# Moving the bfloat16 conversion of quantised x, with its row sums, from ScalarE to one accumulating VectorE instruction per token tile

## Chip, cores and metric

The kernel runs on one core of one Trainium2 chip. The metric is the device time in microseconds from launch to end, as the median of several runs of the same program. One more execution is recorded by the hardware profiler; the views quoted below come from it.

The engines are called PE (TensorE matmuls; PEld is its weight load), DVE (VectorE), ACT (ScalarE), POOL (GpSimd) and SP (SyncE, which only issues transfers here).

## The reference

Input x is 2 x 1024 x 2048 in float32, ctx is 2 x 2048 x 2048. There are two layers with residuals:

```
q(t, s, z) = (clip(round(t / s + z), 0, 255) - z) * s
x = x + q(layernorm(x), s1, z1) @ q(ctx, s2, z2)
z = layernorm(x)
x = x + z @ W + bias + per-group LoRA(z) + shared LoRA(z)
```

The second layer has a 2048 x 2048 weight W, and eight groups of 256 tokens whose LoRA matrices are mixed by a gate.

The kernel forms the first product on centred integers. With c1 = q-integer of x minus 128 and c2 = q-integer of ctx minus 128, it computes c1 @ c2 in bfloat16 (both fit exactly) and corrects for zero points other than 128: a column term from the sums of c2, and a row term from the sums of c1 over a token's 2048 features. The row sums are what accompanies the changed conversion.

## The kernel before, in words

The two batches are done one after the other. Tokens of a batch are eight tiles of 128 rows (`MT = 8`); two tiles make a group of 256 tokens (`MG = 2`, four groups), whose x stays in SBUF as `y[g]` throughout.

**Preparing a tile of x**, `prep_x(b, m, ...)`: DVE takes statistics in four pieces (`st1`, L279), a chain of 128x1 operations makes mean and reciprocal deviation (L253 to L265, with a square root on ACT, L257), then a scale `k` and an offset `o` (L283 to L286). ACT quantises the whole 128 x 2048 tile to uint8, `q8` (L291). ACT then converts `q8` to centred bfloat16, `qh`, in two halves of 1024 columns, each writing its row sums into a column of `rsum` (L294). PE transposes each half in eight 128 x 128 blocks into a PSUM tile (`pt`, L299), and DVE copies that into the operand `c1T` (L300). DVE adds the two row sums (L303) and multiplies by a constant into `r_s` (L304). `q8` alternates between two places in the working buffer `wk`, by parity of m; `qh` has only one place there. `pt`, the column term's `pc` and other small PSUM tiles share a pool of two buffers (`ps_m`).

**Preparing ctx**, `quantise`: ACT scales and rounds a 128 x 2 x 512 piece to int16 (L310), DVE clips and centres it to bfloat16 (L313). Eight pieces make one block of 512 columns. `column_term` sums them on PE (L327) and DVE scales the sums (`bp`, L329).

**The product**, `xattn_pair(b, n, g)`: for each of the two tiles of a group ACT preloads a PSUM accumulator with column term plus row term (L340, needs `r_s`), PE runs 16 matmuls on it (L342), and then DVE scales and adds the accumulator to `y` (L351) and takes statistics for the second layer norm (L353). Three accumulators rotate. Sixteen pairs make a batch's first layer.

**The second layer** (`ffn`) is computed in float32 with two nested seven-product schemes (L580), with operands combined on DVE and POOL and the results added to `y` (L598). While batch 0's last stage of it runs, `meanwhile` already loads and prepares tiles 0 to 3 of batch 1 and the first two column blocks of ctx. Tiles 4 to 7 of batch 1 are prepared after it, between the first pairs of batch 1.

**Order of the work.** Each engine executes its instructions in the order in which it got them. The order is settled ahead of the run by the framework's planner, which takes the order of the program text as priority and works with estimated durations; the preload L340 is marked as of high priority. Loads of x and ctx are issued from SP, in a list (`todo`) that moves on as buffers are given back after L310. Semaphores between engines are made by the framework from the tiles that instructions read and write.

Of the kernel before, what the change touches and what calls it, by code (L numbers as in the profile page):

```python
# [10 lines left out]
F32 = mybir.dt.float32  # L11
# [3 lines left out]
AF = mybir.ActivationFunctionType  # L15
ALU = mybir.AluOpType
# [4 lines left out]
P = 128  # L21
# [5 lines left out]
CENTRE = 128.0  # L27
# [39 lines left out]
def tile_quant_xattn_then_lora_ffn(  # L67
# [17 lines left out]
    nc = tc.nc  # L85
    B, S, D = x.shape
    KT = D // P
    MT = S // P
# [9 lines left out]
    H = D // 2  # L98
# [5 lines left out]
    small = ctx.enter_context(tc.tile_pool(name="small", bufs=4))  # L104
# [21 lines left out]
    r_s = const.tile([P, MT], F32, tag="r_s", name="r_s")  # L126
# [13 lines left out]
    def flat(t):  # L140
        return t.rearrange("p k n -> p (k n)")
# [67 lines left out]
    s12, d1, d2, kdd = (k_s[:, i : i + 1] for i in range(4))  # L209
    n_centre = const.tile([P, 1], F32, tag="n_centre", name="n_centre")  # L210
# [39 lines left out]
    def norm_stats(stats, name):  # L250

        mv = small.tile([P, 2], F32, tag="mv", name=f"mv_{name}")
        nc.vector.bn_aggr(mv, stats.rearrange("p n s -> p (n s)"))  # L253
        ve = small.tile([P, 1], F32, tag="ve", name=f"ve_{name}")
        nc.vector.tensor_scalar_add(ve, mv[:, 1:2], EPS)
        sd = small.tile([P, 1], F32, tag="sd", name=f"sd_{name}")
        nc.scalar.activation(sd, ve, AF.Sqrt)  # L257
        r0 = small.tile([P, 1], F32, tag="r0", name=f"r0_{name}")
        nc.vector.reciprocal(r0, sd)

        t = small.tile([P, 1], F32, tag="nt", name=f"nt_{name}")
        nc.vector.scalar_tensor_tensor(t, ve, r0, r0, ALU.mult, ALU.mult)
        nc.vector.tensor_scalar(t, t, -0.5, 1.5, ALU.mult, ALU.add)
        rstd = small.tile([P, 1], F32, tag="rstd", name=f"rstd_{name}")
        nc.vector.tensor_mul(rstd, r0, t)  # L265
        return mv[:, 0:1], rstd
# [6 lines left out]
    def prep_x(b, m, c1T, wk):  # L273

        nm = f"{b}_{m}"
        g, tok = m // MG, ds((m % MG) * P, P)
        ym = y[g][:, m % MG, :]
        for n in range(NN):
            nc.vector.bn_stats(st1[:, m, n, :], ym[:, ds(n * NB, NB)])  # L279
        mean, rstd = norm_stats(st1[:, m], f"a{nm}")  # L280

        k = small.tile([P, 1], F32, tag="kx", name=f"kx_{nm}")
        nc.vector.tensor_mul(k, rstd, inv1)  # L283
        o = small.tile([P, 1], F32, tag="ox", name=f"ox_{nm}")
        nc.vector.tensor_mul(o, mean, k)
        nc.vector.tensor_sub(o, z1, o)  # L286

        wf = flat(wk)
        q8 = wf[:, ds((m % 2) * (D // 4), D // 4)].bitcast(U8)
        qh = wf[:, D // 2 : D].bitcast(BF16)  # L290
        nc.scalar.activation(q8, ym, AF.Identity, bias=o, scale=k)  # L291
        rsum = small.tile([P, 2], F32, tag="rsum", name=f"rsum_{nm}")
        for h in range(2):
            nc.scalar.activation(  # L294
                qh[:, ds(h * H, H)], q8[:, ds(h * H, H)], AF.Identity, bias=n_centre, accum_out=rsum[:, h : h + 1]
            )
            pt = ps_m.tile([P, KH, P], BF16, tag="pm", name=f"pt_{nm}_{h}")
            for kt in range(KH):
                nc.tensor.transpose(pt[:, kt, :], qh[:, ds(h * H + kt * P, P)], ident_h)  # L299
            nc.vector.tensor_copy(c1T[g][:, ds(h * KH, KH), tok], pt)  # L300

        r_c = small.tile([P, 1], F32, tag="r_c", name=f"r_c_{nm}")
        nc.vector.tensor_add(r_c, rsum[:, 0:1], rsum[:, 1:2])  # L303
        nc.vector.tensor_mul(r_s[:, m : m + 1], r_c, d2)  # L304

    def quantise(c2, r):

# [334 lines left out]
    for b in range(B):  # L642
# [6 lines left out]
        if b == 0:  # L649
            open_c2(0)  # L650
            prep_x(0, 0, c1T, wk)
            for r in range(NR):
                quantise(c2[0], r)
                if r == 3:
                    prep_x(0, 1, c1T, wk)
            for m in range(4, MT):
                load_x(0, m)
            open_c2(1)
            column_term(b, 0, c2[0])
        xattn_pair(b, 0, 0, c1T, c2[0])  # L660
        if b == 0:
            for r in range(4):
                quantise(c2[1], r)
            for m in (2, 3):
                prep_x(b, m, c1T, wk)
# [190 lines left out]
```

## Time and profile before

| | |
|---|---|
| median of 3 runs | 1165.02 us (1162.49 to 1169.69) |
| the profiled execution's own time | 1166.81 us |
| its span, first to last instruction | 1165.0 us |
| PE busy | 1088.4 us (93%), 3747 matmuls |
| DVE busy | 740.7 us (64%) |
| ACT busy | 261.2 us (22%) |
| POOL busy | 285.3 us (24%) |
| quantising x on ACT, L291 | 16 x 2084 ns |
| first matmul of the first layer, L342 | at 42.60 us |
| preparation of batch 0's tiles | up to about 104 us |
| preparation of batch 1's tiles 0 to 3, then 4 to 7 | inside 516 to 600 us, then 623 to 673 us |

Busy times are sums over instructions of the profiled execution. In rows of groups, the text after the first bar is the total busy time and the mean duration of one instruction in ns; after the second bar comes the time that the engine stood idle just before such instructions, and what ended most of it. "A <- B" means written by an instruction that reads B, or, in a list of waits, A waiting for B. An engine's busy share is an average over stages with different limits.

### The profile page before, as it was taken

The page shows a single profiled execution, that of the slowest core. Times are in us where ns is not written, and L with a number is a line of the kernel's source. Part 1 is how long each engine was busy: PE and PEld are TensorE (multiplying, and loading weights), DVE is VectorE, ACT ScalarE, POOL GpSimd, SP SyncE. Part 2 cuts the span into 40 slices and gives each one's busy share as a digit, 9 for nine tenths or more (in the row PEclk, how much of TensorE's full clock was granted, in tenths as well). Part 3 has the DMA queues.
Part 4 walks back from the last instruction along what each step waited for, and adds up shares of the span by engine and source line. Part 5 has one row for each costly group of instructions (what it writes and reads, how often), then busy time and mean ns, then how long its engine had stood idle before and what let it go on. Part 6 is the DMA issues. An engine that isn't in the chain of part 4 may idle for free.

```text
span 1165.0 us, 10275 instructions
## 1 busy us (share of the span) xinstructions
PE 1088.4 (93%) x3747; PEld 487.3 (42%) x3782; DVE 740.7 (64%) x961; ACT 261.2 (22%) x342; POOL 285.3 (24%) x105
## 2 busy tenths in 40 slices
PE   1689999999999989998997999999999999999998
PEld 0344435543433434443443543455343443444443
DVE  4685448665867586669635564676668577674941
ACT  5875413210100000001743661232000000000000
POOL 0000000344445312435000000020634343153600
PEclk9999999999999999998998999999999999999999
DMA  8982937786696745488775074587786774739411
GB/s 308 382 224 70 274 120 254 250 316 233 236 309 231 281 145 206 177 322 314 244 249 209 1 217 127 193 312 253 249 292 243 285 267 169 259 138 327 178 55 54
DMA packets 119619, 261.33 MB, mean 224 GB/s; under 512 B 11792, under 2 KB 16016, under 8 KB 117392
## 3 DMA queue, kind: packets, MB, share of 16 engines
q1 hardware_dynamic: 98112, 218.65, 54.4%
q10 hardware_dynamic: 21456, 42.02, 10.2%
q8 instruction: 30, 0.49, 0.2%
q14 instruction: 21, 0.17, 0.0%
HBM read 224.99 MB, written 37.75 MB: 226 GB/s over the span
## 4 chain that ended last, share of the span: by engine, by line
PE 51%; DMA 22%; DVE 14%; ACT 6%; issue 5%; POOL 2%; SPq 1%; ACTq 0%; DVEq 0%; POOLq 0%
PE fu L580 18%; PE pa L342 12%; PE fv L580 10%; DMA big<-in_w_dram 8%; DVE big L524 4%; PE fw L580 4%; DMA y<-in_x_dram 3%; DMA lit<-in_ctx_dram 3%; DMA bd<-q2b 3%; DVE y L598 2%; DVE big L515 2%; ACT q2b L310 2%; DMA zs<-lit 2%; DMA lit<-zs 2%; PE pc L327 2%
## 5 line engine op out<-in xcount | busy, mean ns | idle before, releaser
L580 PE MATMUL fu<-big,lit 128*128 128x512 f32 x896 | 395.2, 594 | 2.1 <-POOL lit L524 1.4
L524 POOL TENSOR_TENSOR lit<-lit,lit 128x1024 f32<-128x1024 f32 x56 | 174.8, 3130 | 565.5 <-PE px L428 206.7
L580 PEld LDWEIGHTS fu<-big,lit 128*128 128x128 f32 x896 | 167.9, 190 | 215.3 <-issue 208.6
L342 PE MATMUL pa<-big,big 128*128 128x512 bf16 x994 | 232.8, 381 | 17.4 <-ACT pa L340 14.2
L580 PE MATMUL fv<-big,lit 128*128 128x512 f32 x448 | 204.2, 610 | 10.3 <-DVE y L598 10.2
L515 POOL TENSOR_TENSOR lit<-lit,lit 128x1024 f32<-128x1024 f32 x40 | 109.9, 2749 | 276.6 <-DMA lit<-zs 254.2
L524 DVE TENSOR_TENSOR big<-big,big 128x2048 f32<-128x2048 f32 x56 | 162.0, 2905 | 19.8 <-DMA big<-in_w_dram 17.6
L342 PEld LDWEIGHTS <-big 128*128 128x128 bf16 x1024 | 97.9, 98 | 147.8 <-issue 41.8
L515 DVE TENSOR_TENSOR big<-big,big 128x2048 f32<-128x2048 f32 x40 | 103.0, 2575 | 86.6 <-DMA big<-in_w_dram 86.6
L598 DVE TENSOR_TENSOR y<-y,fu 128x1024 f32<-128x1024 f32 (+1 forms) x98 | 114.2, 1192 | 58.6 <-PE fu L580 58.3
L580 PEld LDWEIGHTS fv<-big,lit 128*128 128x128 f32 x448 | 86.4, 195 | 124.0 <-issue 108.2
L458 ACT COPY pl<-bias 128x1024 f32<-128x1024 f32 x32 | 32.6, 1017 | 360.8 <-DVE y L471 289.2
L580 PE MATMUL fw<-big,lit 128*128 128x512 f32 x224 | 99.6, 596 | 0.0
L351 DVE SCALAR_TENSOR_TENSOR y<-pa,k_s,y 128x1024 f32<-128x1024 f32 x32 | 41.0, 1282 | 79.3 <-PE pa L342 79.3
L310 ACT ACTIVATE q2b<-lit,sc,inv 128x1024 int16<-128x1024 f32 x64 | 76.6, 1230 | 49.7 <-DMA lit<-in_ctx_dram 25.9
L598 DVE TENSOR_TENSOR y<-y,fv 128x1024 f32<-128x1024 f32 x48 | 57.0, 1214 | 43.6 <-PE fv L580 43.5
L340 ACT ACTIVATE pa<-bp,r_s 128x512 f32<-128x512 f32 x64 | 42.8, 683 | 99.0 <-DVE y L351 36.5
L580 PEld LDWEIGHTS fw<-big,lit 128*128 128x128 f32 x224 | 41.7, 190 | 54.9 <-issue 54.9
L279 DVE BATCH_NORM_STATS2 st<-y 128x6 f32<-128x512 f32 x64 | 41.1, 678 | 19.8 <-DMA y<-in_x_dram 19.8
L313 DVE TENSOR_SCALAR big<-q2b 128x1024 bf16<-128x1024 int16 x64 | 26.1, 422 | 39.5 <-ACT q2b L310 36.3
L471 DVE TENSOR_TENSOR y<-pl,y 128x512 f32<-128x512 f32 x64 | 41.0, 681 | 8.4 <-PE pl L461 8.3
L299 PE MATMUL pt<-ident_h,big 128*128 128x128 bf16 x256 | 19.9, 230 | 27.9 <-ACT big L294 27.6
(75 smaller groups left out, 599.8 us busy)
## 6 DMA issues: line engine op xcount, KB each, us to landing
big<-in_w_dram SPq DMA_DIRECT2D x96, 1024.0 KB
lit<-zs SPq DMA_DIRECT2D x88, 512.0 KB
lit<-in_ctx_dram SPq DMA_DIRECT2D x64, 512.0 KB
y<-in_x_dram SPq DMA_DIRECT2D x16, 1024.0 KB
out_dram<-y ACTq DMA_DIRECT2D x30, 512.0 KB
zs<-lit ACTq DMA_DIRECT2D x24, 512.0 KB
lit<-in_lora_a_dram SPq DMA_DIRECT2D x32, 256.0 KB
lit<-in_lora_bt_dram SPq DMA_DIRECT2D x32, 256.0 KB
```

Source lines behind the costliest of these rows:

```text
L279: nc.vector.bn_stats(st1[:, m, n, :], ym[:, ds(n * NB, NB)])
L310: nc.scalar.activation(qi, t, AF.Relu, bias=z2, scale=inv2)
L313: nc.vector.tensor_scalar(c2[r // 4][:, ds(2 * (r % 4), 2), :], qi, QMAX, CENTRE, ALU.min, ALU.subtract)
L340: nc.scalar.activation(pa[:, j, :], colt[n], AF.Identity, bias=r_s[:, m : m + 1])
L342: nc.tensor.matmul(pa[:, j, :], c1T[g][:, k, ds(j * P, P)], c2[k // 8][:, k % 8, :], start=False, stop=(k == KT - 1), skip_group_check=True,)
L351: nc.vector.scalar_tensor_tensor(yp, pa, s12, yp, ALU.mult, ALU.add)
L458: nc.scalar.copy(pl, self.bb.unsqueeze(1).to_broadcast([P, 2, NB]))
L471: nc.vector.tensor_add(yb, pl[:, i, :], yb)
L515: eng.tensor_tensor(got[0], got[0], got[1], ALU.add if terms[1][2] > 0 else ALU.subtract)
L524: eng.tensor_tensor(out_t, at[p], at[q], op)
L580: nc.tensor.matmul(ps[:, m, :], at[:, k, ds(m * P, P)], bt[:, k, :], start=(opens and k == 0), stop=(ends and k == KQ - 1), skip_group_che ...
L598: nc.vector.tensor_tensor(yp, yp, chains[chain][:, js, :], ALU.add if sign > 0 else ALU.subtract)
```

## The change

The conversion from `q8` to `qh` is done by one DVE `tensor_scalar` over all 2048 columns, which subtracts the centre, adds 0 and accumulates the row sums into one column of `rsum`. This holds for all tiles of batch 0 and for tiles 4 to 7 of batch 1. Tiles 0 to 3 of batch 1 keep the two ACT instructions. Where DVE converts, the addition of two partial row sums (L303) falls away, since there is only one.

```diff
         nc.scalar.activation(q8, ym, AF.Identity, bias=o, scale=k)
         rsum = small.tile([P, 2], F32, tag="rsum", name=f"rsum_{nm}")
+
+        on_dve = b == 0 or m >= MT // 2
+        if on_dve:
+            nc.vector.tensor_scalar(qh, q8, CENTRE, 0.0, ALU.subtract, ALU.add, accum_out=rsum[:, 0:1])
         for h in range(2):
-            nc.scalar.activation(
-                qh[:, ds(h * H, H)], q8[:, ds(h * H, H)], AF.Identity, bias=n_centre, accum_out=rsum[:, h : h + 1]
-            )
+            if not on_dve:
+                nc.scalar.activation(
+                    qh[:, ds(h * H, H)], q8[:, ds(h * H, H)], AF.Identity, bias=n_centre, accum_out=rsum[:, h : h + 1]
+                )
             pt = ps_m.tile([P, KH, P], BF16, tag="pm", name=f"pt_{nm}_{h}")
             for kt in range(KH):
                 nc.tensor.transpose(pt[:, kt, :], qh[:, ds(h * H + kt * P, P)], ident_h)
             nc.vector.tensor_copy(c1T[g][:, ds(h * KH, KH), tok], pt)
 
-        r_c = small.tile([P, 1], F32, tag="r_c", name=f"r_c_{nm}")
-        nc.vector.tensor_add(r_c, rsum[:, 0:1], rsum[:, 1:2])
-        nc.vector.tensor_mul(r_s[:, m : m + 1], r_c, d2)
+        if on_dve:
+            nc.vector.tensor_mul(r_s[:, m : m + 1], rsum[:, 0:1], d2)
+        else:
+            r_c = small.tile([P, 1], F32, tag="r_c", name=f"r_c_{nm}")
+            nc.vector.tensor_add(r_c, rsum[:, 0:1], rsum[:, 1:2])
+            nc.vector.tensor_mul(r_s[:, m : m + 1], r_c, d2)
```

## The prediction, made before the result was known

> **What bounds the kernel now.** I read the page's engine shares first, then the stages, then who waits for whom. TensorE is busy 93% of the span, so time can come only from stretches where it stands idle. This is the view by stages (columns: stage, its length, then busy time of PE, PEld, DVE, ACT, POOL with instruction counts, granted clock, DMA share, GB/s); the stages are those in which x tiles are prepared by the changed lines.
>
> ```profile
> 0.00:20.00 20.00, 2.74 (x6) 0.74 (x6) 7.48 (x31) 5.90 (x6) 1.17 (x9) 1.00 0.71 264
> 20.00:40.00 20.00, 8.27 (x44) 4.84 (x46) 13.22 (x37) 17.93 (x21) 0.00 (x0) 1.00 1.05 397
> 40.00:60.00 20.00, 15.52 (x92) 7.61 (x93) 13.38 (x39) 18.27 (x22) 0.00 (x0) 1.00 1.03 366
> 60.00:80.00 20.00, 16.85 (x85) 7.88 (x86) 16.79 (x55) 15.61 (x21) 0.00 (x0) 1.00 0.86 220
> 80.00:106.00 26.00, 25.50 (x150) 12.61 (x152) 13.64 (x29) 11.79 (x18) 0.00 (x0) 1.00 0.19 65
> 640.00:660.00 20.00, 19.50 (x112) 9.76 (x114) 11.58 (x40) 15.39 (x20) 0.00 (x0) 1.00 0.00 1
> 660.00:680.00 20.00, 19.84 (x113) 9.06 (x113) 12.12 (x21) 9.05 (x11) 0.00 (x0) 1.00 0.11 32
> ```
>
> From 20 to 60 us ACT is the busiest compute engine (90%), with DVE at two thirds. From 80 us on, and in the second batch from 640, PE is almost full. Next, the waits of PE before 120 us (columns: total us, times, longest):
>
> ```profile
> PE pt L299 <- ACT big L294: 27.6, 2, 19.7
> PE pa L342 <- ACT pa L340: 6.6, 6, 1.7
> ...
> PE pa L342 <- DVE big L300: 1.1, 1, 1.1
> ```
>
> The first row is the start: PE has nothing before the first x tile is converted. The second row is what ACT holds up once matmuls run: the preloads of PSUM (L340), 6.6 us in six waits; together with the copy L300 that is 7.7 us. In the second batch the same waits are 0.3 us, at 658, beside one of 6.8 us at 632.7. That one follows the landing of x at 627.1 and is over before any changed line runs. Then the costs, from the groups with their shapes kept apart (busy us, mean ns of one):
>
> ```profile
> L294 ACT ACTIVATE big<-big,n_centre 128x1024 bf16<-128x1024 uint8 x32 | 36.3, 1136 | 11.9 <-PE pt L299 10.9 <-DVE y L598 0.8
> L294 ACT ACTIVATION_READ_ACCUMULATOR big<-big,n_centre 128x1 f32 x32 | 6.0, 187 | 0.0
> L303 DVE TENSOR_TENSOR r_c<-rsum 128x1 f32<-128x1 f32 x16 | 2.5, 155 | 11.5 <-ACT big L294 11.5
> L471 DVE TENSOR_TENSOR y<-pl,y 128x512 f32<-128x512 f32 x64 | 41.0, 681 | 8.4 <-PE pl L461 8.3
> L313 DVE TENSOR_SCALAR big<-q2b 128x1024 bf16<-128x1024 int16 x64 | 26.1, 422 | 39.5 <-ACT q2b L310 36.3
> ```
>
> **What the Trainium skill says.** "VectorE: DVE Perf Modes", section "The perf-mode tier table", gives tensor_scalar 4x on 16-bit and 2x on 32-bit data in SBUF. The trace agrees for 16 bits: L313 treats 1024 elements in 422 ns, 0.26 ns each if 155 ns (L303's, for one element) is the fixed part. But "SBUF — State Buffer", section "Who interferes with whom", excepts "the form that also writes out its accumulator" from the two-port modes, and "VectorE", section "Two Vector instructions with no wait between them", calls an accumulating operation two instructions, the main one and an accumulator read. Nothing in the trace before is such a DVE instruction. For ACT, "ScalarE: Activation LUTs", section "What ACT_TABLE_LOAD costs", has 280 ns + 0.833 ns per element with a per-partition bias, 1133 ns for 1024; the trace has 1136.
>
> **The change, part by part.** Batch 0's eight tiles and tiles 4 to 7 of batch 1 move, twelve in all; tiles 0 to 3 of batch 1 stay on ACT.
>
> *Removed from ACT:* two conversions and two accumulator reads a tile. In the timeline the first tile's run from 22.37 us to 24.63, so 2.26 us (neighbours overlap a little). Twelve tiles: 27.1 us. *Removed from DVE:* L303, 155 ns a tile.
>
> *Added to DVE:* one conversion of 2048 elements. Price at one element a cycle: 512 elements cost 681 ns (L471) and 1024 cost 1214 ns (L598's full tiles), so 533 ns per 512; 2048 cost 1214 + 2 x 533 = 2280 ns. Add an accumulator read of about 155 ns, an estimate from the one-element rows: 2.43 us. Lower bound, if it did run two a cycle: 1067 + 155 + 155 = 1.38 us. Upper bound: 2.5 us with a dearer read; POOL, which by the same "SBUF" section shares DVE's second port pair, is idle in all these stages. I take 2.43, since the skill excepts this form. Net 2.28 us a tile, 27 us in all: work leaves one engine and arrives on the other, almost equal.
>
> *Order and waits.* Before, the first eight transposes start after one half, 1.1 us into the conversion; now all sixteen wait for 2.3 to 2.4 us. The last eight start as before. qh is a single buffer, so the DVE conversion of the next tile waits for all sixteen transposes of this one, and an in-order DVE keeps what lies behind it: L351 (frees an accumulator of PSUM for L340), L300 (gives PE its operand), L329. Before, it was ACT that waited so: 5.5 us in two waits between 40 and 120 us. No DMA is added or moved; POOL and SP get nothing new. Freed lit buffers follow L310 on ACT, so context loads may be issued slightly earlier; DMA share is 1.03 to 1.05 from 20 to 60 us, so this buys nothing there.
>
> *Stage 0 to 42.6 us, tiles 0 and 1.* From 14.8 to 37 us ACT stands still for only 0.6 us. Tile 0's 2.26 us leave the path to tile 1's quantising (L291, at 29.25 us). DVE, however, gets 2.43 us just when it does tile 1's statistics chain (L253 to L286), so L291 starts between 0.7 and 1.8 us earlier. Tile 1 then converts in 2.43 us instead of the 3.3 us that its two ACT halves took with the L310 ahead of them (31.33 to 34.62), but its first transposes no longer overlap it: about 0.5 us lost. The column term L327 cannot overtake them: its PSUM tile comes from the same pool of two as the transposes' tiles. Gain 0.2 to 1.3 us, taken as 0.7.
>
> *Stage 42.6 to 106 us, tiles 2 to 7.* Of PE's waits on L340, 1.08 us (at 72.56) and 0.29 us (at 89.53) lie behind L294 on ACT in the timeline: gain 1.4 us. The others lie behind L329 or behind L310 and L291: up to 6.3 us more, if a freer ACT shortens them too; I count none. DVE gets 6 x 2.28 = 13.7 us on top of 43.8 us busy of 66: 87%. The cover: DVE idles there 12.6 us ahead of L351 alone (waiting for PE), and 4.1 us ahead of L303 (waiting for L294). But from 51.6 to 70.5 us the chain of waits runs through DVE without a gap. One conversion in six standing in front of a release, at half its length: +1.1 us. Bounds: 0, and 6 x 2.28 = 13.7 us if every one holds PE, as would happen without that idle time.
>
> *Stage 636 to 676 us, tiles 4 to 7 of batch 1.* ACT relief: 0.3 us. DVE idles 12.8 us ahead of L351, against 9.1 us added: half a hit, +0.6; bounds 0 and 9.1.
>
> *Tiles 0 to 3 of batch 1* and the rest of the program: nothing; from 106 to 600 us PE is fed by other things.
>
> Sum: -0.7 - 1.4 + 1.1 - 0.3 + 0.6 = -0.7 us. From the profiled execution's 1166.8 us (span 1165.0, 1.8 around it) this gives 1166.1; the median of the runs shown, 1165.0, is 1.8 below that execution, so the median after is 1164.3, say 1164.
>
> **Rivals.**
>
> *DVE becomes the bound (slower).* Place: batch 0 between 46 and 106 us, and 636 to 676. Mechanism: a 2.4 us conversion, waiting for the previous tile's transposes, sits ahead of L351 or L300, and PE then waits for L340 or for the copied operand. For it: the gapless DVE chain from 51.6 to 70.5, and the planned order, which is settled ahead of the run. Against it: 21 us of DVE idle time in that stage. If half of the ten passes hold PE for their length, 5 x 2.28 = 11.4, less the gains of 2.4: +9, 1174. It decides from two full hits on (4.6 against 2.4). All ten: 1185.
>
> *ACT's relief comes through (faster).* The waits on L340 and L300 in batch 0 (7.7 us) and the 1.3 us of the start shrink by half or more, with the DVE work in its gaps: -4 to -9, about 1159. For it: ACT at 90% from 20 to 60 us. Against: several of these waits are the plain sequence PE, DVE, ACT, PE (L327, L329, L340, L342), which stays. A conversion at 1.38 us would push here, 1.05 us less DVE work a tile.
>
> *The relief is real but swallowed (no difference).* x and context saturate DMA until 60 us, and PE is full from 80 us. Within 1 us of 1165; in the forecast's range.
>
> *The planned order shifts.* The order on each engine is made from estimated durations; another one could move the 6.8 us wait at 632.7 either way: 1158 or 1172.
>
> **How the numbers follow.** Forecast with the swallowed case 0.56 (own range 1160 to 1169); DVE as bound 0.22; ACT's relief 0.14; order 0.08, split evenly. The range 1155 to 1177 leaves out the deep ends of the second and third. A difference over 1%, 11.7 us, is about what a measurement of this kernel can tell from none. Faster by that needs more than the relief case's 9 us: 0.06. Slower needs over six full hits beyond the gains: 0.11. The rest, 0.83, lies within.
>
> **What would show it.** A DVE conversion of about 2.28 us with a short read behind it; ACT's total down from 261 to about 234 us and DVE's up from 741 to about 768; PE's waits on L340 before 120 us at 4 to 7 us; the first L342 between 41.3 and 42.4 us instead of 42.6. Long waits of PE on L351, L300 or L329 would show the first rival; the first L342 well below 41 us, and PE's busy time from 40 to 80 us well above 32.4, the second. A conversion at 1.2 us would refute the price.

## The result, and the profile after

The change made the kernel slower: 1177.5 us median (1176.1 to 1188.8, four runs) against 1164.5 us, a ratio of 1.0111 with a 95% interval of 1.0068 to 1.0154. The forecast was 1164 us; the first rival, DVE as the bound, had 1174. The profiled execution took 1176.7 us, its span is 1174.9 us.

The lines after the inserted ones have moved: L313 to L351 of before are L321 to L359, L300 is L305, L304 is L308, ACT's conversion L294 is L299, and the DVE conversion is L296. The view of groups, shapes apart, of the kernel after shows it as two instructions:

```profile
L296 DVE TENSOR_SCALAR_CACHE_REDUCE big<-big 128x2048 bf16<-128x2048 uint8 x12 | 27.3, 2276 | 4.0 <-ACT big L291 4.0
L296 DVE DVE_READ_ACCUMULATOR big<-big 128x1 f32 x12 | 1.0, 82 | 0.0
```

2276 + 82 = 2358 ns a tile, against 2430 forecast. ACT's busy time fell from 261.2 to 234.9 us (forecast 234), DVE's rose from 740.7 to 764.9 us (forecast 768). The stages of before, in the kernel after (columns as before):

```profile
20.00:40.00 20.00, 9.06 (x48) 5.32 (x49) 15.55 (x36) 11.81 (x11) 0.00 (x0) 0.55 1.04 396
40.00:60.00 20.00, 13.84 (x85) 6.79 (x85) 17.37 (x42) 16.01 (x15) 0.00 (x0) 1.00 1.04 369
60.00:80.00 20.00, 17.67 (x75) 7.58 (x73) 17.98 (x53) 10.71 (x12) 0.00 (x0) 0.91 0.75 206
80.00:106.00 26.00, 25.11 (x150) 12.46 (x148) 20.14 (x32) 6.85 (x9) 0.00 (x0) 1.00 0.19 62
640.00:660.00 20.00, 18.38 (x104) 8.98 (x103) 16.31 (x43) 11.16 (x11) 0.00 (x0) 0.94 0.01 1
660.00:680.00 20.00, 18.89 (x103) 8.86 (x102) 13.32 (x18) 2.88 (x5) 0.00 (x0) 1.00 0.00 1
```

By the third and the fourth busy time of each row, DVE is now busier than ACT in all of these stages, at 87 to 90% from 40 to 80 us, and ACT has time to spare. The granted clock was 0.55 from 20 to 40 us in this profile, against 1.00 in the kernel before; in two further profiles of the change it was 1.00 there, and batch 0 lost the same time as here, batch 1 more (table below), so the clock is not the cause. The waits of PE before 120 us have not shrunk (the preloads and the copies stood at 6.6 and 1.1 us before):

```profile
PE pt L304 <- DVE big L296: 28.7, 4, 19.9
PE pa L350 <- ACT pa L348: 7.0, 5, 2.3
PE pa L350 <- DVE big L305: 1.8, 1, 1.8
```

**Where the time went, by landmarks.** I took from each trace three pieces between engines: from the span's start to the first preload of an accumulator (41.9 us before); from there to the eighth scale-and-add of a pair (L351 before, L359 after; 81.0 us); and from the first scale-and-add of batch 1 to its sixteenth (148.6 us). The table gives the difference to the first profile of before, in us, for every kernel that ran, and the ratio to the runs of before on the same chip. "Rest" is the remainder of the span, the middle (eighth pair of batch 0 to first pair of batch 1) and the end together, where the kernels are almost alike.

| kernel | start | batch 0 | batch 1 | sum | rest | ratio (95%) |
|---|---|---|---|---|---|---|
| before, 2nd profile | -0.2 | 0.0 | +0.6 | +0.3 | +9.6 | |
| before, 3rd | +0.8 | 0.0 | +0.5 | +1.3 | +6.3 | |
| the change | -1.1 | +3.2 | +4.5 | +6.6 | +3.3 | 1.0111 (1.0068 to 1.0154) |
| the change, 2nd | -0.6 | +3.2 | +6.1 | +8.7 | +4.0 | 1.0110 (1.0064 to 1.0157) |
| the change, 3rd | -2.0 | +3.2 | +5.1 | +6.3 | +7.5 | |
| DVE in halves | -1.6 | +5.0 | +4.6 | +7.9 | +0.5 | 1.0066 (1.0039 to 1.0093) |
| batch 0 only | -1.5 | +3.2 | 0.0 | +1.8 | +4.3 | 1.0043 (1.0018 to 1.0069) |
| batch 1 only | -0.8 | 0.0 | +6.4 | +5.6 | +4.5 | 1.0046 (1.0020 to 1.0073) |
| tiles 0, 1 only | -2.4 | +3.9 | +0.1 | +1.7 | +0.9 | 1.0024 (0.9999 to 1.0050) |
| no row sums | -3.3 | -1.4 | +7.0 | +2.3 | +2.2 | 0.9968 (0.9944 to 0.9993) |
| load added to before | -0.8 | +3.9 | +2.9 | +6.0 | +3.1 | 1.0052 (1.0031 to 1.0073) |
| two qh buffers | -1.0 | +4.1 | +2.9 | +6.0 | -1.1 | 1.0034 (1.0010 to 1.0057) |
| one half each | -2.6 | +2.0 | +1.8 | +1.1 | +6.5 | 1.0008 (0.9978 to 1.0038) |
| row sums on ACT | -2.4 | +2.2 | +6.3 | +6.1 | +10.6 | 1.0091 (1.0053 to 1.0128) |
| chain first | -1.5 | +6.9 | +7.9 | +13.3 | +12.0 | 1.0159 (1.0095 to 1.0224) |
| half each, two qh | -4.0 | +3.1 | +1.2 | +0.3 | +7.0 | 1.0026 (1.0006 to 1.0047) |
| before, two qh | -1.2 | +2.0 | +0.4 | +1.3 | -0.1 | 1.0031 (1.0004 to 1.0057) |

Three profiles of one kernel agree to 0.05 us in batch 0 and to some 1.7 us in batch 1, while "rest" differs by up to 9.6 us between profiles of the unchanged kernel. So the 3.3 us of "rest" in the first comparison of two traces say nothing.

**The waits themselves, batch 0.** The first scale-and-add comes at 51.58 us before and at 51.44 us after. From there the timeline of DVE shows no idle time until 73.1 us before, and until 77.3 us after. In this row stands the scaling of a column term (L329 before, L337 after), which the preload and then PE wait for. First before, then after, from the timelines (start, length, idle before and who ended it):

```profile
65.42 0.81 DVE L329 TENSOR_SCALAR bp<-pc,k_s 128x512 f32<-128x512 f32 x1
67.00 4.48 PE L342 MATMUL pa<-big,big 128*128 128x512 bf16 x20 [1.69 <-ACT pa L340]
```

```profile
55.02 2.27 DVE L296 TENSOR_SCALAR_CACHE_REDUCE big<-big 128x2048 bf16<-128x2048 uint8 x1
...
66.86 0.79 DVE L337 TENSOR_SCALAR bp<-pc,k_s 128x512 f32<-128x512 f32 x1
...
68.42 12.21 PE L350 MATMUL pa<-big,big 128*128 128x512 bf16 x48 [2.33 <-ACT pa L348]
```

Tile 3's conversion is now part of that row, and the scaling comes 15.4 us after the first scale-and-add instead of 13.8. The start's gain of 1.1 us is used up and turned into a loss of 1.4 us by then. Tile 7's conversion adds a wait of 1.05 us at 106.61 us, with 0.78 us on a preload at 117.45 us.

**The waits themselves, batch 1.** In batch 1 the waits of PE from 645 to 715 us, in the kernel before and then after:

```profile
658.35 5.56 PE L342 MATMUL pa<-big,big 128*128 128x512 bf16 x24 [0.29 <-ACT pa L340]
...
683.87 0.63 PE L383 MATMUL pga<-ident,q2b 128*128 128x128 f32 x4 [0.42 <-DVE q2b L375]
...
695.94 6.20 PE L342 MATMUL pa<-big,big 128*128 128x512 bf16 x27 [0.22 <-ACT pa L340]
```

```profile
654.96 3.61 PE L350 MATMUL pa<-big,big 128*128 128x512 bf16 x16 [1.62 <-ACT pa L348]
...
679.66 1.07 PE L304 MATMUL pt<-ident_h,big 128*128 128x128 bf16 x16 [1.05 <-DVE big L296]
...
690.49 0.59 PE L350 MATMUL pa<-big,big 128*128 128x512 bf16 x2 [0.78 <-ACT pa L348]
...
704.77 5.56 PE L350 MATMUL pa<-big,big 128*128 128x512 bf16 x25 [1.81 <-ACT pa L348]
```

They add to 0.9 us before and to 5.3 us after. When comparing times in batch 1, take off 3.7 us: the first scale-and-add there comes at 629.98 us before and at 633.69 us after, with what batch 0 and the middle had lost. The first wait: ACT's preload stands in the queue behind the quantising of tiles 5 and 6.

```profile
649.64 4.08 ACT L291 ACTIVATE big<-y,ox,kx 128x2048 uint8<-128x2048 f32 x2 [0.36 <-DVE ox L286]
653.62 1.28 ACT L348 ACTIVATE pa<-bp,r_s 128x512 f32<-128x512 f32 x2
```

In the kernel before that pair of L291 ran at 642.62 us, 12.6 us after the first scale-and-add, and the preload still came in time; now it runs 15.9 us after it. It waits for offsets (L286) that DVE made behind tile 4's conversion (644.11 to 646.4) and behind L361. The second wait is for tile 7's conversion, and that the last two go with it is suggested by the experiment with two qh buffers, where they vanish or shrink together. DVE around it, after:

```profile
674.33 1.28 DVE L359 SCALAR_TENSOR_TENSOR y<-pa,k_s,y 128x1024 f32<-128x1024 f32 x1 [3.26 <-PE pa L350]
675.53 0.68 DVE L305 COPY big<-pt 128x1024 bf16<-128x1024 bf16 x1
676.13 1.27 DVE L361 BATCH_NORM_STATS2 st<-y 128x6 f32<-128x512 f32 x2
677.33 2.27 DVE L296 TENSOR_SCALAR_CACHE_REDUCE big<-big 128x2048 bf16<-128x2048 uint8 x1
...
680.32 1.29 DVE L305 COPY big<-pt 128x1024 bf16<-128x1024 bf16 x2 [0.52 <-PE pt L304]
681.71 1.29 DVE L321 TENSOR_SCALAR big<-q2b 128x1024 bf16<-128x1024 int16 x3
```

DVE stood idle for 3.26 us just before, but could not convert tile 7 in that time: PE did the last transposes of tile 6, which read the only qh, at 674.13. Then the conversion stood behind L359, L305 and L361 in the queue, until 677.33. In the kernel before, ACT had converted tile 7's first half at 664.57 and waited only with the second, on an ACT that had nothing else to do:

```profile
664.57 1.13 ACT L294 ACTIVATE big<-big,n_centre 128x1024 bf16<-128x1024 uint8 x1
...
668.57 1.15 ACT L294 ACTIVATE big<-big,n_centre 128x1024 bf16<-128x1024 uint8 x1 [2.77 <-PE pt L299]
```

L313 followed at 674.37. Now its successor L321 comes at 681.71, that is 7.3 us later, of which 3.7 us were there at the first scale-and-add. The context pieces are quantised later by as much, their buffers come free later, and SP issues the next context loads at 683.44 us in place of 676.10. At 704 us the preload L348 stands behind a quantising that waits for a load of context:

```profile
702.90 1.24 ACT L318 ACTIVATE q2b<-lit,sc,inv 128x1024 int16<-128x1024 f32 x1 [0.85 <-DMA lit<-in_ctx_dram]
704.04 0.67 ACT L348 ACTIVATE pa<-bp,r_s 128x512 f32<-128x512 f32 x1
```

So one late DVE instruction returns as a wait for DMA some 25 us on.

### The profile page after: what moved, and what is told of

The parts are those of the page before. It is cut to its first block, busy times and chain, and to the rows that moved or that the text cites. A ratio compares the mean times of both kernels' runs of the same rounds, so it can differ in the third digit from the quotient of the medians.

```text
span 1174.9 us, 10261 instructions
## 1 busy us (share of the span) xinstructions
PE 1089.0 (93%) x3782; PEld 486.3 (41%) x3782; DVE 764.9 (65%) x973; ACT 234.9 (20%) x294; POOL 288.9 (25%) x105
## 4 chain that ended last, share of the span: by engine, by line
PE 54%; DMA 21%; DVE 15%; issue 4%; ACT 3%; POOL 2%; SPq 1%; ACTq 0%; DVEq 0%; POOLq 0%
PE fu L588 19%; PE pa L350 13%; PE fv L588 10%; DMA big<-in_w_dram 8%; PE fw L588 5%; DMA lit<-in_ctx_dram 4%; DMA lit<-zs 3%; DVE big L532 3%; DMA zs<-lit 3%; DVE big L523 2%; DVE y L606 2%; PE pc L335 2%; DMA bd<-q2b 2%; DVE big L296 1%; PE ptz L420 1%
## 5 line engine op out<-in xcount | busy, mean ns | idle before, releaser
L532 POOL TENSOR_TENSOR lit<-lit,lit 128x1024 f32<-128x1024 f32 x56 | 179.2, 3208 | 574.3 <-DMA zs<-lit 422.0
L350 PE MATMUL pa<-big,big 128*128 128x512 bf16 x1024 | 238.3, 385 | 22.0 <-ACT pa L348 20.0
L588 PE MATMUL fv<-big,lit 128*128 128x512 f32 x448 | 199.5, 598 | 7.6 <-DVE y L606 7.4
L523 POOL TENSOR_TENSOR lit<-lit,lit 128x1024 f32<-128x1024 f32 x40 | 109.2, 2731 | 274.2 <-DMA lit<-zs 251.6
L359 DVE SCALAR_TENSOR_TENSOR y<-pa,k_s,y 128x1024 f32<-128x1024 f32 x32 | 41.0, 1281 | 72.4 <-PE pa L350 72.4
L348 ACT ACTIVATE pa<-bp,r_s 128x512 f32<-128x512 f32 x64 | 43.1, 685 | 125.7 <-PE pa L350 35.1
L321 DVE TENSOR_SCALAR big<-q2b 128x1024 bf16<-128x1024 int16 x64 | 25.8, 420 | 32.6 <-ACT q2b L318 32.4
L304 PE MATMUL pt<-ident_h,big 128*128 128x128 bf16 x256 | 19.1, 231 | 30.0 <-DVE big L296 29.8
L469 PE MATMUL pl<-bp,axT 64*128 64x512 f32 x128 | 38.4, 641 | 9.1 <-ACT pl L466 9.0
```

Source lines behind the costliest of these rows:

```text
L321: nc.vector.tensor_scalar(c2[r // 4][:, ds(2 * (r % 4), 2), :], qi, QMAX, CENTRE, ALU.min, ALU.subtract)
L348: nc.scalar.activation(pa[:, j, :], colt[n], AF.Identity, bias=r_s[:, m : m + 1])
L350: nc.tensor.matmul(pa[:, j, :], c1T[g][:, k, ds(j * P, P)], c2[k // 8][:, k % 8, :], start=False, stop=(k == KT - 1), skip_group_check=True,)
L359: nc.vector.scalar_tensor_tensor(yp, pa, s12, yp, ALU.mult, ALU.add)
L469: nc.tensor.matmul(pl[:, i, :], axT[rows, pr, ds(j * P, P)], self.bp[rows, :], start=False, stop=True, skip_group_check=True,)
L523: eng.tensor_tensor(got[0], got[0], got[1], ALU.add if terms[1][2] > 0 else ALU.subtract)
```

## The experiments

**Which place.** Four kernels that change only part of it. In halves: two `tensor_scalar` calls of 1024 columns inside the loop over h, and the addition of two sums. The others change one line:

```diff
-        on_dve = b == 0 or m >= MT // 2
+        on_dve = b == 0                      # batch 0 only
+        on_dve = b == 1 and m >= MT // 2     # batch 1 only
+        on_dve = b == 0 and m < 2            # tiles 0, 1 only
```

DVE in halves: 

> Both halves are converted on DVE by two accumulating instructions of 1024 columns (about 1.2 us each and a read each; one more DVE add of the two sums returns). The computation is complete. DVE gets about 0.4 us a tile more than with one instruction. Theory A (the grain: transposes wait for the whole conversion, and the next conversion for all sixteen transposes): most of the loss goes, 1166 to 1170 us. Theory B (DVE's load as such: 2.3 us more a tile ahead of the releases): no better than the change, 1176 to 1182 us. Theory C (a chance of the planned order): anywhere, with waits at new places.

Batch 0 only: 

> DVE converts the eight tiles of batch 0 alone; batch 1 is as before. By the traces batch 0 stands 1.1 us ahead at the first product and 2.0 us behind at its end. All theories, if places add up: 2 to 3 us over before, about 1167 us. If the loss seen in batch 1 is a late consequence of batch 0's shift (transfers that fall otherwise), it stays: 1172 us or more.

Batch 1 only: 

> DVE converts tiles 4 to 7 of batch 1 alone. By the traces the stage from 623 to 700 us lost 6.5 us, of which 2.0 us came with a later landing of x. Grain or load theory: 4 to 7 us over before, about 1170 us. If the loss there is handed down from batch 0: within 1 us of before.

Tiles 0 and 1 only: 

> DVE converts tiles 0 and 1 of batch 0 alone, where ACT was busy without a gap and PE has nothing to do. Prediction's step on the start: first product 1.1 us earlier as in the change, nothing lost later: 1163 to 1164.5 us. If the gain at the start is swallowed by the later order: 1165 us or more.

Batch 0 alone costs 1.0043 and batch 1 alone 1.0046, together 0.9% against the change's 1.1%, within the intervals. Each has its own loss in its one profile (+3.2 and +6.4 us) and none in the other batch: the places add up, and no loss in batch 1 is handed down from batch 0. Halves give 1.0066. Each half takes 1212 + 83 ns, so DVE has 0.23 us a tile more (and L303 again). The interval overlaps that of the change, and the landmark sum, 7.9 us, is no smaller than the change's 6.3 to 8.7. So a part for the grain is not shown, and "most of the loss", as theory A had it, did not go. The start gains 2.4 us when only tiles 0 and 1 move, and then batch 0 loses 3.9 us: the planner put five context quantisings ahead of tile 3's L291 on ACT, and PE waited 4.16 us for tile 3's conversion. Here the gain at the start is swallowed by the next arrangement of the queues.

**Load, waits, or both.** Without the accumulator (a zero in place of the sums); a load of the same size in the kernel before; two qh buffers, for which q8 gives up one of its two places; one half on each engine (`tensor_scalar` for the first half, `activation` for the second, edit not printed):

```diff
-            nc.vector.tensor_scalar(qh, q8, CENTRE, 0.0, ALU.subtract, ALU.add, accum_out=rsum[:, 0:1])
+            nc.vector.tensor_scalar(qh, q8, CENTRE, 0.0, ALU.subtract, ALU.add)
+            nc.vector.memset(rsum[:, 0:1], 0.0)
```

```diff
 # in the kernel before, same twelve tiles
+        if b == 0 or m >= MT // 2:
+            extra = small.tile([P, 1], F32, tag="extra", name=f"extra_{nm}")
+            nc.vector.tensor_scalar(axT.rearrange("p a t -> p (a t)").bitcast(U8), q8, 0.0, 0.0, ALU.subtract, ALU.add, accum_out=extra)
```

```diff
-        q8 = wf[:, ds((m % 2) * (D // 4), D // 4)].bitcast(U8)
-        qh = wf[:, D // 2 : D].bitcast(BF16)
+        q8 = axT.rearrange("p a t -> p (a t)").bitcast(U8)
+        qh = wf[:, ds((m % 2) * (D // 2), D // 2)].bitcast(BF16)
```

No row sums: 

> As the change, but the DVE conversion has no accumulator; the row sums are left out (a zero stands in for them, so the row term is not computed). The waits between the engines are the same. If the conversion without accumulator takes about half the time (1.2 us for 2.27 + 0.08): theory B (load of DVE ahead of the statistics chain and the releases) expects about half the loss back, 1.005 times before; theory A (grain and single buffer) expects about the same third to half, since the waits get shorter too; theory C (order by chance) anything.

Load without waits: 

> The kernel before, with ACT converting as ever, and for the same twelve tiles one more DVE instruction of the same form and length (2048 elements, accumulator) that reads the quantised tile and writes to an unused buffer; nobody reads its result. Theory B (load): DVE's queue alone brings most of the loss, 1.006 to 1.010 times before, with PE waiting for L340 behind late L291 on ACT. Theory A (waits on the conversion): within 0.3% of before.

Two qh buffers: 

> As the change, but qh has two buffers by parity of the tile (q8 has one, placed in a buffer that is free at those times), so a conversion need not wait for the transposes of the tile before. Complete computation. Theory A (single qh): PE's waits on the conversion of tile 7 (1.05 us in each batch) go and the loss shrinks to 1.003 to 1.006 times before. Theory B: within 0.2% of the change, 1.009 to 1.012.

One half each: 

> For the same tiles DVE converts the first half and ACT the second (each with its accumulator). Complete computation. DVE gets 1.3 us a tile in place of 2.36, ACT keeps 1.3 us of 2.26. Theory B: about half the loss, 1.004 to 1.006 times before. Theory A (grain): transposes start after 1.3 us again and the first half no longer waits for the other: 1.000 to 1.003. If the balance of the two engines at the start counts, slightly faster than before.

The load alone, whose result nobody waits for, costs 1.0052, a little under what theory B expected, and 6.0 us of the landmark sum: theory A as the only cause falls. The added instruction took 2281 + 84 ns. It also reads q8, which a later tile's L291 overwrites, but no idle time of L291 in the profile ended with it. PE's waits from 638 to 710 us became:

```profile
PE pa L345 <- ACT pa L343: 2.5, 4, 1.2
PE pt L302 <- DVE big L303: 1.2, 1, 1.2
PE pga L386 <- DVE q2b L378: 0.4, 1, 0.4
```

The first two rows are preloads and a copy held up by a queue, as theory B said; the third was there before. Without the accumulator the conversion takes half the time, and the loss is gone (0.9968), more than theory B expected:

```profile
L296 DVE TENSOR_SCALAR big<-big 128x2048 bf16<-128x2048 uint8 x12 | 14.6, 1220 | 3.8 <-ACT big L291 3.8
```

In its one profile the batch 1 piece is nevertheless 7.0 us longer. 5.3 us of it lie in one place: having come to batch 1's first pair 7.5 us early, ACT stood at context loads (2.92 and 2.21 us) with the preload behind them, and PE waited 5.33 us for it at 694.26.

Two qh buffers bring the change to 1.0034, within theory A's range. Tile 7's conversion in batch 1 then runs at 660.79 us, and its copies end at 677.0 instead of 681.6:

```profile
660.79 2.27 DVE L296 TENSOR_SCALAR_CACHE_REDUCE big<-axT 128x2048 bf16<-128x2048 uint8 x1
...
675.73 1.27 DVE L305 COPY big<-pt 128x1024 bf16<-128x1024 bf16 x2
```

The waits of 1.05, 0.78 and 1.81 us are gone in batch 1 (0.22 us is left of the last), the first two in batch 0 too. In return a preload at 83.26 us waits 1.69 us instead of 0.39, and a transpose at 653.23 waits 2.62 us for a copy L305, so the landmark sum drops only from about 7 to 6.0 us: less in batch 1 (2.9 against 4.5 to 6.1), more in batch 0 (4.1 against 3.2). The ratio fell by more than the landmarks show; where the difference lies is not known. One half each is the same as before within its interval (1.0008).

**Other ways out.** Row sums by an ACT pass over q8 of its own, with the fast DVE conversion (the centre, which that pass does not subtract, is then taken off the sum by one more small DVE operation); and the statistics chain ahead of the conversions:

```diff
+            nc.vector.tensor_scalar(qh, q8, CENTRE, 0.0, ALU.subtract, ALU.add)
+            nc.scalar.activation(
+                axT.rearrange("p a t -> p (a t)").bitcast(U8), q8, AF.Identity, bias=0.0, accum_out=rsum[:, 0:1]
+            )
...
+            nc.vector.tensor_scalar_add(r_c, rsum[:, 0:1], -CENTRE * D)
```

```diff
-        mean, rstd = norm_stats(st1[:, m], f"a{nm}")
+        with tc.high_priority():
+            mean, rstd = norm_stats(st1[:, m], f"a{nm}")
... # k and o likewise
```

Row sums on ACT: 

> As the change, but DVE converts without accumulator (1.22 us, as measured without the row sums), and ACT makes the row sums in a pass of its own over the quantised tile (2048 elements, about 2.2 us, for which only L348 waits, by way of r_s). Complete computation. Theory B (DVE's load): as good as without row sums, 0.995 to 1.000 times before. If ACT's relief was what made that run fast: 1.000 to 1.005, with the first product near 42 us.

Chain first: 

> As the change (one accumulating DVE conversion a tile, complete computation), but the chain of small statistics operations (L253 to L286) has high priority in the planner, so that it stands ahead of conversions on DVE where both are ready. DVE's load is the same. If the loss comes from conversions standing ahead of the next tiles' chain (late L291 on ACT, and L348 behind it): half of it or more goes, 1.003 to 1.006 times before, and the wait of 1.6 us on L348 at about 655 us is gone. If it is load as such: as the change, 1.009 to 1.012.

The change again: 

> The change itself once more, beside runs of before on this chip: 1.007 to 1.015 times before by the first comparison. The profile shows how much of a difference of two traces is chance: the waits between engines from 40 to 120 us and from 638 to 710 us should repeat to within 0.3 us each, those on transfers of weights and context not.

With the sums on ACT it is 1.0091, above both expected ranges, although DVE converts in 1218 ns: the pass takes 1897 + 187 ns of ACT in the same queue as L348 and L291, and PE waited 4.06 us for a conversion at 53.18 and 3.40 us for L348 at 706.61. So time taken off DVE is worth little if it is laid on ACT; the fast run without row sums had both engines relieved against the change. The amount of work alone does not settle the loss: here ACT was busy for 257.5 us and DVE for 753.4, with the load added to before 261.6 and 766.4, and the latter lost no more (1.0052). Chain first was the worst, 1.0159, beyond both of its ranges, in four runs from 1178 to 1193 us. The wait it was aimed at went from 1.62 to 1.35 us only, and new ones came (3.37 and 2.23 us on L348 at 68.30 and 77.18). The planner still put tile 4's conversion before the last steps of the chain of tiles 5 and 6, so the thought that the chain's place decides is neither shown nor refuted; as a remedy it failed. The change again repeats its 1.0110, with the same waits of PE to within 0.1 us except the last (2.49 against 1.81), which ends with a DMA.

**The control, a last attempt, and how far chance goes.**

Half each, two qh: 

> First half of each tile on DVE, second on ACT, as in the run with one half each, and qh in two buffers (q8 in one). Complete computation. It puts both suspects together at their cheapest: 1.3 us of DVE a tile and no wait for the transposes of the tile before. If load and single buffer are the two parts of the loss: 0.995 to 1.000 times before. If the order of the work decides more than either: 1.000 to 1.005.

Before with two qh: 

> The kernel before (ACT converts) with two qh buffers and one q8: the control for the run of the change with two qh buffers. Complete computation. If the second buffer helps only where a whole-tile DVE conversion waits: 0.998 to 1.002 times before. If it helps any form: 0.993 to 0.997, and then the gap between the change and its version with two buffers says nothing of the change itself.

Before, second profile: 

> The kernel before, unchanged, for a second profile. Its waits between engines from 40 to 130 us and 638 to 715 us should be those of the first profile to within 0.3 us each. Open is the second layer of batch 1 (after 800 us): there every changed kernel stood 0.1 to 7 us longer than the first profile of before, though none touches it. If that is chance in transfers of weights, this profile is 2 to 5 us longer there too.

Before, third profile: 

> As the second profile of before: the same engine waits; the second layer's waits on transfers tell how far chance goes there.

The change, third profile: 

> The change for a third profile: engine waits as in the other two; if the landing of x at about 625 us is later than before's by chance alone, it falls among the three profiles of before here.

Two buffers do not help the kernel before (1.0031, so slightly slower, which neither expectation had), so what they give back to the change belongs to the change. Both remedies together are no faster than before (1.0026), the second of the two expected ranges. No version with complete sums beat it. The repeated profiles show how far chance goes in the "rest": the kernel before itself stood 6.3 and 9.6 us longer there than in its first profile, as much as the change's 3.3 to 7.5. The engine waits of before repeated up to 125 us and from 645 to 715 us; a preload at about 128 us, which waited 0.32 us at first, waited 1.60 us in the second profile.

## Why the prediction was wrong

*Prices: right.* 2276 + 82 ns against 2280 + 155 forecast; the rate of the lower bound exists too, but only without the accumulator (1220 ns). The Trainium skill's exception for the accumulating form, in "SBUF — State Buffer", section "Who interferes with whom", agrees with the trace: 1.11 ns an element with the accumulator, 0.60 without.

*The start: right in sign, a little small.* First L342 at 41.5 us, within the 41.3 to 42.4 named; mean of three profiles 1.2 us earlier than the first of before, 1.4 earlier than the mean of three, against 0.7 with bounds of 0.2 and 1.3. The three profiles of before differ by 1.1 us in this piece.

*Batch 0's stage: wrong.* The step was "One conversion in six standing in front of a release, at half its length: +1.1 us", with ACT's relief of 1.4 us against it, -0.3 in sum. Measured: +3.2 us in all three profiles. The relief did come (of the waits at 72.56 and 89.53 only 0.39 us on L348 is left, at 81.92), but others grew or were added: 2.33 us on L348 at 68.42 (1.69 before), 1.83 on L305 (1.09 before), 1.05 on the conversion of tile 7. The prediction had seen that DVE has no gap from 51.6 to 70.5 us, and still charged half of one conversion for the whole stage. What the planner put into this row came ahead of the column term's scaling, 1.6 us later than before, and PE waited for it. That this is load, and not the single qh, three runs say: the load added to before, which no one waits for, loses 3.9 us in this piece, the change with two qh buffers 4.1, and the conversion of half the length, without sums, gains 1.4.

*Tiles 4 to 7 of batch 1: wrong by more.* "DVE idles 12.8 us ahead of L351, against 9.1 us added: half a hit, +0.6", with 0.3 of relief. Measured: 4.5, 6.1 and 5.1 us, less 0.4 for the mean of before: +4.9.

The second term, and in part the first, counted DVE's idle time as cover for the new work. That idle time lies ahead of L351, while DVE waits for a product of PE. The conversion cannot use it when its own input is not there, as tile 7's in batch 1, whose qh is still being read by tile 6's transposes, or when it stands behind L359 in the queue. It then runs after the wait, in the row of L359, L305, L361, and pushes the next steps: offsets for L291, clipping of context, and by those ACT's preload and SP's next loads. The prediction had named the single qh and the in-order queue, and gave them the price of half an instruction. The experiments show two contributions. One is DVE time as such: a load with no reader costs 0.5%, and half the conversion's time, with the sums left out, takes the whole loss away. The other is the wait on the single qh: two buffers take the change from 1.1 to 0.3%, and do not help before. In the one profile with two buffers the second is seen in batch 1 only, where 4.5 to 6.1 us become 2.9, the same 2.9 that the load alone costs there. The two are not cleanly additive: each edit also lets the planner arrange the queues anew, so a single profile of an edit is no exact price of its cause.

*The rival that came* was the first; its size, +9 us, was nearer than the forecast, and the median lies half a microsecond beyond the range. Its mechanism is the one seen: a conversion ahead of other DVE work, and PE waiting for the preload or the copied operand. Its threshold of two full hits was reached by several partial ones, which the count of "hits" had left out.

*What stays open.* The three pieces between engines give -1.4 + 3.2 + 4.9 = +6.7 us, and the ratio says 12.9 us, with 7.9 as the lower end of its interval. No cause is shown for the missing 1 to 6 us. The "rest", where three profiles of each kernel overlap, does not hold them either: on average the three spans of the change are 6.3 us longer than those of before. The medians too depend on few runs: the kernel before had 1164.5 us in the four runs of the result and 1169.3 to 1170.6 in the later sets of 11 to 69; the ratio was 1.011 both times that the change ran beside it. Whether the chain's place on DVE is a third contribution was not told apart.

## What to carry to other kernels

Idle time of an engine that works through a queue in order covers new work only where that work's inputs are there when the idle time begins, and where the queue lets it run then: look at what the engine is waiting for, and what the new instruction waits for, before counting it. Where a stretch has no idle time and others wait for what stands in it, count new work as a delay of what stands behind it: here 2.27 us of conversion put off a release by 1.6. Moving work between two helper engines of almost equal price gained nothing here, where both feed the same loop, and a form that halves the speed for the sake of a side result, such as an accumulator, should be priced against leaving that result out. For tile 7 of batch 1 the single qh kept ACT waiting for 2.8 us, and ACT had time to spare; on DVE the wait reached PE.

## What the runs showed of the hardware

The accumulating DVE tensor_scalar takes 2276 ns for 2048 uint8 elements into bfloat16 and 1212 ns for 1024, plus an accumulator read of 82 to 84 ns, less than half of ACT's (187 ns). From 1024 to 2048 columns that is 1.04 ns an element. The same conversion without the accumulator takes 1220 ns for 2048, 0.54 of the time, although the source is uint8. Two executions of one program differed by up to 9.6 us in stages that no edit touched, more than most of the edits; what made them differ was not looked into.
